# Two transformer layers on one core: output product, offset and pass order at the start of the last feed-forward

## The chip, the cores and the metric

The kernel runs on one core of a Trainium2 chip. The metric is the device time of one execution in microseconds (us), the median of several runs. The profile shows one further execution: TensorE (PE, with its weight loads PEld), VectorE (DVE), ScalarE (ACT), GpSimd (POOL) and the DMA queues, whose issues stand on SP. Times in the profile are counted from the span's start.

## What is computed

Two layers follow one another over x of shape (2, 512, 512), fp32: two independent chunks of 512 rows. Each half-layer adds its result to x and normalises the rows.

```
x = layernorm(x + linear_attention(x))        # elu features against a fixed memory
x = layernorm(x + ternary_ffn(x))             # int8 truncations
x = layernorm(x + softmax_attention(x))       # one head, d = 128, then Wo
x = layernorm(x + ffn(x))                     # inter = silu(x Wg^T) * (x Wu^T); inter Wd^T
```

The change lies where the third line ends and the fourth begins. There, for each chunk b, out = probs V, then x = x + (out Wo) / sums, then the norm over the 512 columns, then products of x with the 1376 rows of Wg and of Wu, and of the result with Wd.

## The kernel before

All of it is unrolled. A chunk b has four tiles t of 128 rows, kept as `xs[b][t]`, 128 x 512. The columns are cut into four blocks k of 128. The 1376 inner columns are eleven weight chunks j, of which the last to be loaded has 96 columns.

**Order.** Each engine runs its own queue in order. The order on GpSimd is that of the program; on the other engines a planner in the compiler lays the instructions out ahead of time, by the program's order and by the times at which it expects each to be ready, and it may move a later instruction into a gap. `tc.issue_after(ins)` ties the instructions of a block behind `ins` on their engine, without a wait of its own. PSUM is one pool of eight banks (`psum`), a bank for each product.

**The end of the softmax attention.** `output(b, t)` is one product of `ots[b]` with `wo1` into a bank (L910; fp32, two instructions). `attended(b, t, p)` adds the bank, scaled by the row sums, to `xs[b][t]` on VectorE (L915). `norm_a1` of chunk 0 takes statistics on VectorE (L155, L157), then `root` makes the reciprocal deviation on GpSimd (L163, L164), then `scalar_norm` makes the offset -mean x rstd in two GpSimd instructions (L904, L905) and applies both on ScalarE (L906). In the program chunk 0's four products and norms come first, then chunk 1's `values`, then chunk 1's four products and additions; chunk 1's statistics come later.

**Splitting the rows.** Full fp32 accuracy is had from products in a reduced format (fp32r): each operand becomes three parts, h (its upper 12 bits, cut by a mask), l (the rest) and d (a cross term). `split_rows(b, room)` does so for x: for each block k it transposes the four tiles into one bank (L942), copies the bank to SBUF on ScalarE (L948; not for block 0 of chunk 0, which is read from the bank), cuts it on VectorE (`cut`, L729), and `row_parts` makes h on ScalarE (L748) and l and d on VectorE (L749, L750). It returns the last instruction as `done`; behind it are tied the statistics of chunk 1's four tiles, and behind these their normalisation on VectorE (L169).

**The products.** `up1(b, j)` makes gate and up for weight chunk j: h and l products gather in a bank `pm`, d products in `pc` (L1007), for each of gate and up. `run` issues them: for j = 0 block by block, since the parts of x come block by block, otherwise first all d, then all h, then all l. `sum_up` evicts on ScalarE (L1017) and VectorE (L1018); a Silu (L1040) and a product (L1042) follow. The steps begin (0,0), (0,1), (0,2), (1,0), (1,1), (1,2); `split_rows(1, ...)` stands behind step (0,1). `down1` (L1082) makes the last product; its norm is `scalar_norm` too, for all tiles but the last.

Of the kernel before, what the change touches and what calls it, by code (L numbers as in the profile page):

```python
# [15 lines left out]
ALU = mybir.AluOpType  # L16
# [3 lines left out]
P = 128  # L20
B, S, HID = 2, 512, 512
NT = S // P
NK = HID // P
# [13 lines left out]
def kernel(  # L37
# [19 lines left out]
    nc = tc.nc  # L57
# [12 lines left out]
    ident = const.tile([P, P], F32, tag="ident", name="ident")  # L70
# [8 lines left out]
    def psum(name):  # L79
        return ps.tile([P, 512], F32, tag="mm", name=name)  # L80


    xs = [[], []]
# [188 lines left out]
    def split(b):  # L272

        hi = xtp.tile([P, NK, S], F32, tag="xt", name=f"xh_{b}").bitcast(F32R)
        los = [pair_tile(f"xl_{b}_{i}").bitcast(F32R) for i in range(2)]
        his = [hi[:, k, :] for k in range(NK)]
        los = [los[k // 2][:, k % 2, :] for k in range(NK)]

        def block(k):
            pt = psum(f"pt_f0{b}_{k}")  # L280
            for t in range(NT):
                nc.tensor.transpose(pt[:, ts(t, P)], xs[b][t][:, ts(k, P)], ident)
            nc.scalar.copy(his[k], pt)
            nc.vector.tensor_sub(los[k], pt, his[k].bitcast(F32))

        return his + los, block
# [12 lines left out]
    with tc.tile_pool(name="a0w", bufs=1) as a0w, tc.tile_pool(name="a0", bufs=2) as a0:  # L299
# [201 lines left out]
        for i, (b, t) in enumerate(order):  # L501
# [10 lines left out]
            if i == 5:  # L512
                parts, block = split(0)
# [21 lines left out]
    with tc.tile_pool(name="f0", bufs=2) as f0:  # L535
# [83 lines left out]
        pds, ys, stats, moved = {}, {}, {}, {}  # L619
# [42 lines left out]
        parts, block = split(1)  # L662
# [62 lines left out]
    def cut(src, w, name):  # L725

        m = cutp.tile([P, 512], F32, tag="cut", name=f"m_{name}")
        p = src.shape[0]
        nc.vector.tensor_single_scalar(  # L729
            m[:p, :w].bitcast(I32), src.bitcast(I32), TOP12, ALU.bitwise_and  # L730
        )
        return m[:p, :w]
# [12 lines left out]
    def row_parts(src, m, parts):  # L745

        h, l, d = parts
        moved = nc.scalar.copy(h, m)  # L748
        nc.vector.tensor_sub(l, src, m)  # L749
        return moved, nc.vector.scalar_tensor_tensor(  # L750
            d, l.bitcast(F32), -BIG, m, ALU.mult, ALU.add
        )


    turn = [6, 7, 8, 9, 10, 0, 1, 2, 3, 4, 5]
# [7 lines left out]
    def take(n):  # L763
        got = free[:n]
        del free[:n]
        return got

    def split_up(j, room):

        c = turn[j]  # L770
        n = CHUNKS[c][1]
        for a in range(2):
            w = gus[c][:, a].rearrange("p k i -> p (k i)")
            up_parts[j, a] = room[3 * a : 3 * a + 3]
            done = weight_parts(w, up_parts[j, a], f"gu{j}_{a}")
        own = wffn.tile([P, 2 * n // P, 512], F32R, tag=f"gu{c}", name=f"ugu_{c}")
        free.extend(units(own))
        return done
# [15 lines left out]
    for b in range(B):  # L794
# [10 lines left out]
        for j in range(2):  # L805
            p = psum(f"pqk_{b}_{j}")
# [6 lines left out]
            moved = nc.scalar.activation(s, p, AF.Identity, bias=bqk[:, j : j + 1])  # L813
# [4 lines left out]
        for t in range(NT):  # L818
            p = psum(f"pv_{b}_{t}")
# [57 lines left out]
    with tc.issue_after(scaled_max.ins):  # L877
        done = split_up(2, room1[6:] + take(4))
# [7 lines left out]
    def values(b, pt, cuts):  # L886

        ot = ot2[:, b, :]
        w = S // cuts
        for i in range(cuts):  # L890
            po = psum(f"pot_{b}_{i}")
            for k in range(NT):
                nc.tensor.matmul(  # L893
                    po[:, :w], qkv[b][2][:, k, :], pt[:, k, ts(i, w)],
                    start=(k == 0), stop=(k == NT - 1),
                )
            (nc.vector.tensor_copy if b else nc.scalar.copy)(ot[:, ts(i, w)], po[:, :w])
        ots.append(ot)

    def scalar_norm(x, stats, name):  # L900

        mv, rstd = stats
        off = small.tile([P, 1], F32, tag="off", name=f"off1_{name}")
        nc.gpsimd.tensor_tensor(off, mv[:, 0:1], rstd, ALU.mult)  # L904
        nc.gpsimd.tensor_scalar(off, off, -1.0, None, ALU.mult)  # L905
        nc.scalar.activation(x, x, AF.Identity, bias=off, scale=rstd)  # L906

    def output(b, t):
        p = psum(f"po1_{b}_{t}")
        nc.tensor.matmul(p, ots[b][:, ts(t, P)], wo1, start=True, stop=True)  # L910
        return p

    def attended(b, t, p):
        x = xs[b][t]
        nc.vector.scalar_tensor_tensor(  # L915
            x, p, probs[b][1][:, t : t + 1], x, ALU.mult, ALU.add
        )
# [6 lines left out]
    def rows_room(b, name):  # L924

        if b == 0:
            tiles = [
                wop.tile([P, 2, 512], F32R, tag="wo", name=f"{name}_{i}") for i in range(6)
            ]
        else:  # L930
            tiles = [
                xtp.tile([P, NK, S], F32R, tag="xt", name=f"{name}_{i}") for i in range(2)
            ] + [wqp.tile([P, 2, 512], F32R, tag="wq", name=f"{name}_{i}") for i in range(2, 4)]
        return [u for t in tiles for u in units(t)]

    def split_rows(b, room):

        parts, moved = [], []
        for k in range(NK):
            pt = psum(f"pt_f1{b}_{k}")  # L940
            for t in range(NT):
                nc.tensor.transpose(pt[:, ts(t, P)], xs[b][t][:, ts(k, P)], ident)  # L942
            if b or k:
                rows = cutp.tile([P, 512], F32, tag="big", name=f"xt_f1{b}_{k}")
                with ExitStack() as tied:
                    if k > 1:
                        tied.enter_context(tc.issue_after(moved[k - 2].ins))
                    nc.scalar.copy(rows, pt)  # L948
                pt = rows
            with ExitStack() as tied:  # L950
                if b == 0 and k == 1:
                    tied.enter_context(tc.issue_after(done.ins))
                m = cut(pt, S, f"x{b}_{k}")
            parts.append(room[3 * k : 3 * k + 3])
            copied, done = row_parts(pt, m, parts[k])
            moved.append(copied)
        return parts, done

    values(0, pt0, 1)
# [2 lines left out]
        attended(0, t, output(0, t))  # L962
        norm_a1(0, t)
    values(1, pt1, 2)
    for t in range(NT):
        attended(1, t, output(1, t))
    rooms = [rows_room(0, "r0"), None]
    x3 = [None, None]
    x3[0], done = split_rows(0, rooms[0])
    stats1 = []  # L970
    for t in range(NT):
        with tc.issue_after(done.ins):
# [10 lines left out]
    def products(b, j, a):  # L983


        n = CHUNKS[turn[j]][1]
        h, l, d = (u[:, : NK * n].rearrange("p (k i) -> p k i", k=NK) for u in up_parts[j, a])
        pc, pm = psum(f"pc_{b}_{j}_{a}"), psum(f"pm_{b}_{j}_{a}")
        passes = [
            [(w[:, k], x3[b][k][i], (pm, pm, pc)[i]) for i, w in enumerate((h, l, d))]  # L990
            for k in range(NK)
        ]
        return pc[:n], pm[:n], passes

    def run(passes, by_block):

        if by_block:
            todo = [p for block in passes for p in block]
        else:
            todo = [block[i] for i in (2, 0, 1) for block in passes]  # L1000
        begun = {}
        for _, _, p in todo:
            begun[id(p)] = begun.get(id(p), 0) + 1
        left = dict(begun)
        for w, x, p in todo:
            n = w.shape[-1]
            nc.tensor.matmul(  # L1007
                p[:n], w, x, start=(left[id(p)] == begun[id(p)]), stop=(left[id(p)] == 1)
            )
            left[id(p)] -= 1  # L1010

    def sum_up(pc, pm):

        n = pc.shape[0]
        ev = evicted.pop(0)
        evicted.append(ev)
        nc.scalar.activation(ev[:n], pc, AF.Copy, scale=CROSS)  # L1017
        nc.vector.scalar_tensor_tensor(ev[:n], pm, MAIN, ev[:n], ALU.mult, ALU.add)  # L1018
        return ev[:n]
# [3 lines left out]
    def up1(b, j):  # L1023

        n = CHUNKS[turn[j]][1]
        g = j // 4
        if (b, g) not in its:
            its[b, g] = fp.tile(
                [P, GROUPS[g], S], F32, tag=f"it{b}{g}", name=f"it_f1{b}{g}", bufs=1
            )  # L1030
            if g == turn.index(last) // 4:
                nc.gpsimd.memset(its[b, g][96:, turn.index(last) % 4, :], 0.0)
        (pc0, pm0, passes0), (pc1, pm1, passes1) = (products(b, j, a) for a in range(2))
        if j == 0:
            run([p + q for p, q in zip(passes0, passes1)], True)
        else:
            run(passes0, False)
            run(passes1, False)
        gate = sum_up(pc0, pm0)
        nc.scalar.activation(gate, gate, AF.Silu)  # L1040
        wide = sum_up(pc1, pm1)
        nc.vector.tensor_mul(its[b, g][:n, j % 4, :], gate, wide)  # L1042
# [156 lines left out]
```

## Time and profile before

| | |
|---|---|
| median of 3 runs | 476.58 us (475.98 to 476.86) |
| the profiled execution | 475.66 us |
| its span, first to last instruction | 473.8 us |
| mean granted TensorE clock | 0.998 |
| TensorE busy, share of the span | 98% |
| start of the first output product of chunk 1 | 278.58 us |
| last row part of chunk 0 (L750) ends | 289.94 us |
| TensorE's second group of transposes starts | 295.79 us |

A line of the timeline has the start, the length, the engine, the line of the program, the operation, what is written and read, and the shapes; in brackets stands how long the engine had been idle and what released it. Several like instructions in a row are one line with a count. A matmul's recorded end lies past the start of the next one, since they are pipelined; the distance of starts is its price.

### The profile page before, as it was taken

The page shows a single profiled execution, that of the slowest core. Times are in us where ns is not written, and L with a number is a line of the kernel's source. Part 1 is how long each engine was busy: PE and PEld are TensorE (multiplying, and loading weights), DVE is VectorE, ACT ScalarE, POOL GpSimd, SP SyncE. Part 2 cuts the span into 40 slices and gives each one's busy share as a digit, 9 for nine tenths or more (in the row PEclk, how much of TensorE's full clock was granted, in tenths as well). Part 3 has the DMA queues.
Part 4 walks back from the last instruction along what each step waited for, and adds up shares of the span by engine and source line. Part 5 has one row for each costly group of instructions (what it writes and reads, how often), then busy time and mean ns, then how long its engine had stood idle before and what let it go on. Part 6 is the DMA issues. An engine that isn't in the chain of part 4 may idle for free.

```text
span 473.8 us, 5817 instructions
## 1 busy us (share of the span) xinstructions
PE 465.8 (98%) x1891; PEld 328.8 (69%) x1891; DVE 349.5 (74%) x688; ACT 272.6 (58%) x513; POOL 115.1 (24%) x147
## 2 busy tenths in 40 slices
PE   9999999999999999999999999999999999999994
PEld 7454444434488788787766567888788888888884
DVE  1355677677766586756989989998875778999852
ACT  3344899556656877546754934786653666334221
POOL 0353102666540293000365032000000000023221
PEclk9999999999999999999999999999999999999999
DMA  8999700000033000231390000000000000001011
GB/s 304 403 347 357 291 1 1 0 0 1 2 121 119 3 1 13 79 91 36 124 381 2 0 1 1 1 1 0 1 0 1 1 1 1 0 24 43 24 46 44
DMA packets 13748, 33.98 MB, mean 72 GB/s; under 512 B 1872, under 2 KB 2768, under 8 KB 13712
## 3 DMA queue, kind: packets, MB, share of 16 engines
q1 hardware_dynamic: 13280, 32.85, 19.1%
q10 hardware_dynamic: 432, 0.66, 0.4%
q8 instruction: 22, 0.36, 0.3%
q14 instruction: 14, 0.11, 0.1%
HBM read 31.40 MB, written 2.10 MB: 71 GB/s over the span
## 4 chain that ended last, share of the span: by engine, by line
PE 71%; ACT 7%; DVE 5%; issue 3%; POOL 1%; POOLq 0%; DVEq 0%; ACTq 0%
PE pm L1007 17%; PE pg_f L550 9%; PE pc L1007 9%; PE pu_f L550 8%; PE pdm L1082 7%; PE pd_f L606 4%; PE pdc L1082 4%; DVE x L412 4%; PE pqk L808 3%; PE po L390 2%; ACT y L403 2%; ACT t L422 2%; PE pv L821 2%; PE po L910 1%; PE pot L893 1%
## 5 line engine op out<-in xcount | busy, mean ns | idle before, releaser
L390 PE MATMUL po<-mw,q 128*128 128x512 f32 x128 | 57.1, 598 | 0.3 <-DVE mv_a L157 0.2
L345 PE MATMUL pq<-xt_a,wq 128*128 128x512 f32 (+1 forms) x136 | 56.4, 568 | 0.0
L163 POOL TENSOR_TENSOR rstd_f<-mv_f,ln_eps 128x1 f32<-128x1 f32 x15 | 4.3, 287 | 183.3 <-DVE mv_f L1093 130.2
L390 PEld LDWEIGHTS po<-mw,q 128*128 128x128 f32 x128 | 23.0, 189 | 32.1 <-issue 18.0
L345 PEld LDWEIGHTS pq<-xt_a,wq 128*128 128x128 f32 x136 | 25.5, 190 | 27.7 <-issue 25.9
L1007 PE MATMUL pm<-r,it_early 128*128 128x512 f32 x144 | 37.4, 390 | 0.4 <-ACT r L748 0.4
L1007 PE MATMUL pm<-r,ugu 128*128 128x512 f32 (+1 forms) x144 | 36.3, 389 | 0.0
L1007 PEld LDWEIGHTS pm<-r,it_early 128*128 128x128 f32 x144 | 27.0, 188 | 6.3 <-ACT r L748 0.7
L412 DVE SCALAR_TENSOR_TENSOR x<-po,den,x 128x511 f32<-128x511 f32 x40 | 29.8, 745 | 1.9
L1007 PEld LDWEIGHTS pm<-r,ugu 128*128 128x128 f32 (+1 forms) x144 | 26.8, 186 | 5.9
L185 ACT ACTIVATE ta_f<-y_f,below_half 128x512 int8<-128x512 f32 (+1 forms) x22 | 15.9, 723 | 23.8 <-DVE y_f L175 23.3
L1018 DVE SCALAR_TENSOR_TENSOR ev_q<-pm,ev_q 128x512 f32<-128x512 f32 (+1 forms) x28 | 19.1, 685 | 13.4 <-PE pm L1007 13.3
L407 POOL TENSOR_TENSOR y<-y,y 128x511 f32<-128x511 f32 x16 | 20.3, 1270 | 31.5 <-ACT y L403 30.7
L576 DVE SCALAR_TENSOR_TENSOR it_f<-tb_f,ta_f 128x512 fp32r<-128x512 int16 (+1 forms) x22 | 15.2, 690 | 16.2 <-ACT tb_f L186 16.2
L351 ACT ACTIVATE e<-pq,bq 128x512 f32<-128x512 f32 x16 | 11.1, 692 | 25.9 <-PE pq L345 25.9
L1007 PE MATMUL pc<-r,ugu 128*128 128x512 f32 (+1 forms) x96 | 25.8, 391 | 0.0
L424 POOL TENSOR_SCALAR td<-wd,inv_down 128x512 fp32r<-128x512 f32 (+1 forms) x11 | 19.5, 1788 | 24.0 <-DVE inv_down L219 23.8
L550 PE MATMUL pg_f<-xh,tu 128*128 128x512 f32 (+1 forms) x88 | 24.8, 402 | 0.0
L550 PE MATMUL pg_f<-xl,tu 128*128 128x512 f32 (+1 forms) x88 | 23.6, 390 | 0.0
L550 PE MATMUL pu_f<-xh,tu 128*128 128x512 f32 (+1 forms) x88 | 23.6, 390 | 0.0
L550 PE MATMUL pu_f<-xl,tu 128*128 128x512 f32 (+1 forms) x88 | 23.6, 389 | 0.0
L1017 ACT ACTIVATE ev_q<-pc 128x512 f32<-128x512 f32 (+1 forms) x28 | 16.4, 590 | 11.5 <-PE pc L1007 11.3
(293 smaller groups left out, 1103.0 us busy)
## 6 DMA issues: line engine op xcount, KB each, us to landing
gu<-in_gu SPq DMA_DIRECT2D x20, 512.0 KB, 8.2
wo<-in_wo SPq DMA_DIRECT2D x16, 512.0 KB, 6.6
wd<-in_wd SPq DMA_DIRECT2D x20, 256.0 KB, 4.6
wq<-in_wq SPq DMA_DIRECT2D x8, 256.0 KB, 4.2
out<-x SPq DMA_DIRECT2D x7, 256.0 KB, 2.0
x<-in_x SPq DMA_DIRECT2D x6, 256.0 KB, 5.3
gu<-in_gu SPq DMA_DIRECT2D x2, 384.0 KB, 6.6
wqkv<-in_wqkv SPq DMA_DIRECT2D x1, 768.0 KB, 10.7
```

The source lines that it names most:

```text
L185: nc.scalar.activation(a[:n], y, AF.Relu, bias=below_half[:n])
L345: nc.tensor.matmul(pq[:, at], wq[h][:, k, :], xt[:, k, at], start=(k == 0), stop=(k == NK - 1),)
L390: nc.tensor.matmul(po, qs[b][h0 + j][:, ts(t, P)], mw[:, h0 + j, :], start=True, stop=True,)
L407: nc.gpsimd.tensor_add(ys[0][:, :LAST], ys[0][:, :LAST], y[:, :LAST])
L412: steps.append(nc.vector.scalar_tensor_tensor(x[:, :LAST], four[j][:, :LAST], d, x[:, :LAST], ALU.mult, ALU.add))
L424: eng.tensor_scalar(out, w, factor, None, ALU.mult)
L550: nc.tensor.matmul(pp[a][:n], t[:, a, i % NK, :n], x2[b][i], start=(i == 0), stop=(i == 2 * NK - 1),)
L606: nc.tensor.matmul(pd, inter[b][c][:n, ts(t, P)], td[c][:n].bitcast(F32R), start=(c == 0), stop=(c == last),)
L1007: nc.tensor.matmul(p[:n], w, x, start=(left[id(p)] == begun[id(p)]), stop=(left[id(p)] == 1))
L1017: nc.scalar.activation(ev[:n], pc, AF.Copy, scale=CROSS)
L1018: nc.vector.scalar_tensor_tensor(ev[:n], pm, MAIN, ev[:n], ALU.mult, ALU.add)
L1082: nc.tensor.matmul(p[:, :w], got[j // 4][1][kind][:n, j % 4], down_parts[j][kind][:, cols], start=(j == 0 and kind == kinds[0]), stop=(j = ...
```

## The change

Three edits.

- `scalar_norm`: the offset is made by one GpSimd `tensor_scalar`, mean times rstd times -1.
- `split_rows` gets an argument `behind`, two functions. With it, all sixteen transposes are issued first, the blocks tied in order; behind the last of them comes the first function, `output(1, 3)`; and behind block 0's last part on VectorE comes the second, `attended(1, 3, p)`. The loop over chunk 1's tiles ends one earlier. Only chunk 0's call passes `behind`; chunk 1's transposes go on as before.
- For j = 0, the gate's and up's passes of a block alternate: h of gate, h of up, l, l, d, d, where they were h, l, d of gate and then h, l, d of up. This holds for both chunks.

```diff
         mv, rstd = stats
         off = small.tile([P, 1], F32, tag="off", name=f"off1_{name}")
-        nc.gpsimd.tensor_tensor(off, mv[:, 0:1], rstd, ALU.mult)
-        nc.gpsimd.tensor_scalar(off, off, -1.0, None, ALU.mult)
+        nc.gpsimd.tensor_scalar(off, mv[:, 0:1], rstd, -1.0, ALU.mult, ALU.mult)
         nc.scalar.activation(x, x, AF.Identity, bias=off, scale=rstd)
...
-    def split_rows(b, room):
-
-        parts, moved = [], []
+    def split_rows(b, room, behind=None):
+
+
+        parts, moved, pts = [], [], []
+
+        def turn(k):
+            pt = psum(f"pt_f1{b}_{k}")
+            with ExitStack() as tied:
+                if behind and k:
+                    tied.enter_context(tc.issue_after(pts[k - 1][1].ins))
+                for t in range(NT):
+                    turned = nc.tensor.transpose(
+                        pt[:, ts(t, P)], xs[b][t][:, ts(k, P)], ident
+                    )
+            pts.append((pt, turned))
+
+        if behind:
+            for k in range(NK):
+                turn(k)
+            with tc.issue_after(pts[-1][1].ins):
+                p = behind[0]()
         for k in range(NK):
-            pt = psum(f"pt_f1{b}_{k}")
-            for t in range(NT):
-                nc.tensor.transpose(pt[:, ts(t, P)], xs[b][t][:, ts(k, P)], ident)
+            if not behind:
+                turn(k)
+            pt = pts[k][0]
             if b or k:
...
             copied, done = row_parts(pt, m, parts[k])
             moved.append(copied)
+            if behind and k == 0:
+                with tc.issue_after(done.ins):
+                    behind[1](p)
         return parts, done
...
-    for t in range(NT):
+    for t in range(NT - 1):
         attended(1, t, output(1, t))
     rooms = [rows_room(0, "r0"), None]
     x3 = [None, None]
-    x3[0], done = split_rows(0, rooms[0])
+    t = NT - 1
+    x3[0], done = split_rows(
+        0, rooms[0], (lambda: output(1, t), lambda p: attended(1, t, p))
+    )
...
         if j == 0:
-            run([p + q for p, q in zip(passes0, passes1)], True)
+            run([[x for y in zip(p, q) for x in y] for p, q in zip(passes0, passes1)], True)
         else:
```

## The prediction

> **What bounds the kernel now.** I read the page's first part, then the chain of work that ended last, then the timeline of each engine around the change.
>
> ```profile
> PE 465.8 (98%) x1891; PEld 328.8 (69%) x1891; DVE 349.5 (74%) x688; ACT 272.6 (58%) x513; POOL 115.1 (24%) x147
> PE 71%; ACT 7%; DVE 5%; issue 3%; POOL 1%; POOLq 0%; DVEq 0%; ACTq 0%
> ```
>
> TensorE is busy for 98% of the span. So only a stretch in which TensorE stands still can be shortened by reordering, and the chain says where it does: cut to the neighbourhood of the change, in order of time, it leaves TensorE once.
>
> ```profile
> 278.74 3.43 PE po L910 x8
> 282.17 0.12 PE pt_f L942
> 282.30 0.73 DVE x L915
> 283.03 0.61 DVE m_x L729
> ...
> 283.66 0.70 DVE r L749
> ...
> 284.39 0.70 DVE r L750
> ...
> 285.13 0.50 PE pc L1007
> ```
>
> The columns are start, length, and who. The fourth output product ends, VectorE adds it to x (L915), and only then does it cut the first transposed block (L729, L749, L750), for which the feed-forward's first products wait. TensorE's own timeline shows what that costs:
>
> ```profile
> 282.01 1.91 PE L942 MATMUL pt_f<-ident,x 128*128 128x128 f32 x16
> 284.33 0.73 PE L1007 MATMUL pm<-r,it_early 128*128 128x512 f32 x2 [0.41 <-ACT r L748]
> 285.13 0.50 PE L1007 MATMUL pc<-r,it_early 128*128 128x512 f32 x1
> 285.47 0.62 PE L1007 MATMUL pm<-r,it_early 128*128 128x512 f32 x2
> 285.94 0.62 PE L1007 MATMUL pc<-r,it_early 128*128 128x512 f32 x2
> 286.40 1.55 PE L1007 MATMUL pm<-r,it_early 128*128 128x512 f32 x6
> ```
>
> The chain also gives the pace of a dense stream: 8 products in 1.81 to 1.82 us, 0.227 each; 16 transposes in 1.75, 0.109 each; 8 halves of an output product in 3.43, 0.429 each. So the transposes are issued by 282.01 + 1.75 = 283.76 and the first product starts 0.57 later; the seven products before 286.40 would need 1.59 and take 2.07, 0.48 lost, mostly before the product that reads L750's result. Together 1.05 us. From 286.40 to the end of the down products I find no other stop above 0.25 us. **1.05 us is the ceiling.** 0.2% of 476.58 is 0.95 us, about what a measurement of this kernel can tell from no change.
>
> Before that, the fourth norm of chunk 0 is made by GpSimd and ScalarE:
>
> ```profile
> 279.79 0.19 POOL L163 TENSOR_TENSOR rstd_a<-mv_a,ln_eps 128x1 f32<-128x1 f32 x1
> 280.06 0.57 POOL L164 TENSOR_TENSOR rstd_a<-rstd_a,minus_half 128x1 f32<-128x1 f32 x1
> 280.71 0.19 POOL L904 TENSOR_TENSOR off_a<-mv_a,rstd_a 128x1 f32<-128x1 f32 x1
> 280.99 0.22 POOL L905 TENSOR_SCALAR off_a<-off_a 128x1 f32<-128x1 f32 x1
> 281.24 0.81 ACT L906 ACTIVATE x<-x,off_a,rstd_a 128x512 f32<-128x512 f32 x1 [0.56 <-POOL off_a L905]
> ```
>
> x is ready at 282.05, and the transposes start at 282.01: close, hidden by the output product. And 13 us later comes a second meeting of the two chunks:
>
> ```profile
> 294.03 0.55 DVE L169 TENSOR_SCALAR x<-x,mv_a,rstd_a 128x512 f32<-128x512 f32 x1 [0.44 <-POOL rstd_a L164]
> 295.02 0.55 DVE L169 TENSOR_SCALAR x<-x,mv_a,rstd_a 128x512 f32<-128x512 f32 x1 [0.44 <-POOL rstd_a L164]
> 295.79 1.91 PE L942 MATMUL pt_f<-ident,x 128*128 128x128 f32 x16
> ```
>
> The last tile of chunk 1 is normalised at 295.57, and its first transpose (the fourth of 16) is due at 295.79 + 3 x 0.109 = 296.12. That is 0.55 of slack, about 0.45 after the weight load ahead of it.
>
> **The Trainium skill.** "TensorE: Matmul & The Clock Gate", section "LDWEIGHTS (loading the stationary operand)", gives columns / 1.2 ns: 107 ns for 128. The trace agrees in an indirect way: after a wait the second product starts 0.335 after the first, 0.108 over the pace, so a stop costs its length and one uncovered load. "GPSIMD Engine Reference", "Key points", says that GpSimd shares SBUF interfaces with VectorE and suffers from VectorE instructions with two SBUF inputs. The trace agrees: L904 takes 0.19 in this stretch but 2.28 at 441.8, beside such instructions. "VectorE: DVE Perf Modes", "The perf-mode tier table", puts a PSUM source in a slower tier for tensor_scalar: the cut L729 takes 0.68 from PSUM, 0.42 from SBUF, so block 0 keeps the dear one.
>
> **The change, part by part.**
>
> 1. Offset in one GpSimd step. L904 and L905 take 0.28 each from start to start. One tensor_scalar with a per-partition factor has no row here; the nearest is L905, 0.22. Bounds: 0.22, or the old pair, 0.53. I take 0.23, so 0.28 less in each norm. Norms 1 to 3 queue behind one another on GpSimd: norm 1 begins at 277.03 (statistics), then 277.03 + 3 x 1.11 gives 280.36 for the last offset, L906 from 280.42 to 281.23, 0.82 earlier. If the step took 0.53, x would stay at 282.05 and the transposes would lose 0.57 against part 2.
>
> 2. Output product (1,3) behind the transposes. TensorE does the same work, in another order: transposes from 282.01 - 0.86 = 281.15; block 0's fourth at 281.48 finds x ready (281.23); all by 282.90; the product by 283.76. No DMA moves, SP's queue is untouched, and GpSimd only has fewer instructions. VectorE: the third L915 ends at 282.17, so the cut starts at 282.08 instead of 282.95 (0.87 earlier); ScalarE's copy is ready at 283.41, L749 at 283.50, L750 at 284.21. TensorE is free at 283.76, later than the first two, so the 0.57 goes. L915 for (1,3) is put behind L750: 284.13 to 284.86. Behind it on VectorE wait the cuts of blocks 1 to 3: the first at 284.78 instead of 285.00. **So of VectorE's 0.87 only 0.22 is left for everything after block 0.**
>
> 3. Passes by kind (h,h,l,l,d,d for gate and up, where it was h,l,d,h,l,d). Four products, 0.91, now lie before the first d: due at 284.67, ready at 284.21. That takes the other 0.48. In chunk 1 the parts were ready anyway (d of block 0 at 301.03, used from 303.5); gate's last product moves back by two, 0.45, ahead of an eviction that nothing is waiting for then. Cost nothing; without that cover, 0.45.
>
> What is late next: TensorE has done block 0's six products at 285.12, and block 1's h comes at 285.00 - 0.22 + 0.42 + 0.65 = 285.85. That is 0.73, three products of the next weight chunk (their parts for block 0 exist; the plan put two such in gaps before, at 286.17 and 289.16). Block 3's h, at 289.15 - 0.22 = 288.93, leaves another 0.3. With none of these gaps filled, the last of chunk 0's 24 products ends where it does now and the gain is nil; with two fillers 0.43; with five the whole 1.05.
>
> Then the second meeting. If TensorE runs 1.05 ahead, the fourth transpose is due at 295.07; the tile is normalised at 295.57 - 0.22 = 295.35, and with the load's 0.1 TensorE can't be further ahead than 0.45 + 0.22 = 0.67. The plan orders by its own times; it left VectorE's two 0.44 holes before L169 unfilled although evictions were ready, so it seems to take these norms as sooner than they are, and will put the transposes there without other products ahead. **I take 0.65 us**: 475.66 - 0.65 = 475.01 for the profiled execution (span 473.8, 1.86 around it). That execution lies 0.92 below the median of the runs, 476.58; on it the same gain gives 475.9.
>
> **Rivals.**
>
> A. Everything is filled, at the second meeting too (the next chunk's cross products need only chunk 0's parts): gain 0.95 to 1.05, 475.6. For it: the plan filled gaps before. Against it: VectorE's holes.
>
> B. The gaps behind block 0 stay open, because L915 took the place of the wait that it left: gain 0 to 0.4, 476.4. For it: VectorE is behind block 0 nearly as late as now. Against it: fillers exist and PSUM banks are free (transposes 0 to 2 are read by 284.8).
>
> C. Slower. VectorE has no idle moment from 295.0 to 323.9. In it chunk 1's parts are cut 2.0 to 2.4 us before their use; with TensorE 0.65 ahead and VectorE 0.22, 1.6 to 2.0 is left. If the plan, seeing chunk 0's results sooner, lets evictions and gate products go ahead of these cuts, each costs 0.6. Up to three are free; six cost 3.6 - 1.8 = 1.8 of stall, less the 0.65: 477.7. It decides from the fifth on (3.0 - 1.8 - 0.65 = 0.55 slower). Against it: the cuts stand earlier in the program than the evictions that would be freed.
>
> **How the numbers follow.** The forecast 0.38, A 0.34, B 0.11, C 0.17. A reaches the bound of 0.95 us only narrowly: three quarters of it count as faster, with a quarter of the forecast, since the median of three runs scatters by about 0.3: 0.255 + 0.095 = 0.35. Slower is C, nearly whole: 0.16. The rest, 0.49, is within 0.2%. The range takes in A, the forecast and B with 0.4 of scatter between runs: 475.1 to 477.0; C lies outside.
>
> **What would show it.** TensorE's first product at 283.8 without a wait named; L915 once between L750 and the second L729; L905 gone, L904 one instruction of 0.2 to 0.25, the fourth L906 at 280.4. If cross products lie between 285.1 and 285.9, part 2 is filled. If the second transposes start near 295.0 with a stop inside the first four, the forecast; with products of the third chunk ahead of them, A. A first product later than 284.0, or L906 after 281.5, makes the prediction wrong; so does any new wait of TensorE on VectorE between 296 and 324.

## The result, and the profile after

| | before | after |
|---|---|---|
| median of 22 runs each | 476.47 us (475.62 to 476.91) | 475.29 us (474.34 to 477.18) |
| ratio, 95% interval | | 0.9978 (0.9971 to 0.9985) |
| profiled execution | 475.66 us | 474.57 us |
| its span | 473.8 us | 472.8 us |
| granted TensorE clock | 0.998 | 0.999 |

By the ratio the kernel became 1.05 us faster (0.71 to 1.38 by its interval); the two medians differ by 1.18. Forecast were 475.9 us and a gain of 0.65. The sign holds, and so does the mechanism in the stretch around the change; the amount was too small by about 0.4. The page's first part and the shares of the chain say hardly more than that TensorE is still the bound (behind POOL there are eleven instructions less, one for each norm made by ScalarE):

```profile
PE 465.6 (98%) x1891; PEld 328.6 (70%) x1891; DVE 349.5 (74%) x688; ACT 272.5 (58%) x513; POOL 112.7 (24%) x136
...
PE 72%; ACT 7%; DVE 5%; issue 3%; POOL 0%; POOLq 0%; DVEq 0%; ACTq 0%
```

The chain of work around the change, in order of time (start, length, who), no longer leaves TensorE. Where VectorE's L915, L729, L749 and L750 stood in it, there are now the fourth output product and the first products:

```profile
281.27 1.75 PE pt_f L946 x16
283.02 0.86 PE po L909 x2
283.88 0.92 PE pm L1030 x4
284.80 0.69 PE pc L1030 x3
285.50 0.23 PE pm L1030
285.72 0.23 PE pc L1030
285.95 1.84 PE pm L1030 x7
```

The timeline of the same stretch gives the steps one by one (its starts lie about 0.16 ahead of the chain's; the lines moved: L906 is now L905, L910 is L909, L915 is L914, L942 is L946, L1007 is L1030, L1018 is L1041, L1082 is L1105):

```profile
280.18 0.26 POOL L904 TENSOR_SCALAR off_a<-mv_a,rstd_a 128x1 f32<-128x1 f32 x1
280.48 0.81 ACT L905 ACTIVATE x<-x,off_a,rstd_a 128x512 f32<-128x512 f32 x1 [0.32 <-POOL off_a L904]
281.11 1.91 PE L946 MATMUL pt_f<-ident,x 128*128 128x128 f32 x16
282.05 0.68 DVE L729 TENSOR_SCALAR m_x<-pt_f 128x512 int32<-128x512 int32 x1
283.49 0.69 DVE L750 SCALAR_TENSOR_TENSOR r<-r,m_x 128x512 fp32r<-128x512 f32 x1
284.10 0.74 DVE L914 SCALAR_TENSOR_TENSOR x<-po,sums,x 128x512 f32<-128x512 f32 x1
284.76 0.75 DVE L729 TENSOR_SCALAR m_x<-xt_f 128x512 int32<-128x512 int32 x2
285.33 0.39 PE L1030 MATMUL pm<-r,it_early 128*128 128x512 f32 x1
285.56 0.39 PE L1030 MATMUL pc<-r,it_early 128*128 128x512 f32 x1
285.88 1.90 PE L1030 MATMUL pm<-r,it_early 128*128 128x512 f32 x7
```

Before, the cuts of block 0 and of the next two blocks were these:

```profile
282.95 0.68 DVE L729 TENSOR_SCALAR m_x<-pt_f 128x512 int32<-128x512 int32 x1
285.00 0.75 DVE L729 TENSOR_SCALAR m_x<-xt_f 128x512 int32<-128x512 int32 x2
```

x is ready at 281.29, before the fourth transpose (281.11 + 3 x 0.109 = 281.44). The cut starts at 282.05, 0.90 earlier than before; the cuts of the other blocks start at 284.76, 0.24 earlier, because L914 lies between. Block 0's six products and one of the next weight chunk run from 283.72 (the start of the output product's second half, 283.29, and its 0.43) to 285.33, then two more of that chunk; the starts 285.33, 285.56, 285.88 are 0.23 and 0.32 apart and the next one 0.34 behind, so the wait for block 1's h costs 0.10 + 0.11 over the pace of 0.227.

Ten microseconds later the second meeting stands in the timeline of GpSimd, VectorE and TensorE:

```profile
292.90 0.85 POOL L164 TENSOR_TENSOR rstd_a<-rstd_a,minus_half 128x1 f32<-128x1 f32 x1
294.78 0.55 DVE L169 TENSOR_SCALAR x<-x,mv_a,rstd_a 128x512 f32<-128x512 f32 x1 [0.44 <-POOL rstd_a L164]
294.91 2.12 PE L946 MATMUL pt_f<-ident,x 128*128 128x128 f32 x16
296.78 1.17 PE L1030 MATMUL pc<-r,ugu 128*128 128x512 f32 x4
```

The last tile is normalised at 295.33, the fourth transpose was due at 294.91 + 0.33 = 295.24. Sixteen transposes take 296.78 - 294.91 = 1.87 where 1.67 lay between the same starts before (295.79 to 297.46): 0.2 is lost. The product behind the transposes before was

```profile
297.46 1.17 PE L1007 MATMUL pc<-r,ugu 128*128 128x512 f32 x4
```

TensorE comes 0.88 ahead of before and leaves 0.68 ahead; 0.04 of both is an earlier start ahead of the change. From there on it stays 0.67 to 0.70 ahead to its last product.

In the executions compared below, chunk 1's first output product starts anywhere between 278.54 and 280.11, so two stretches are used in place of the span: the **distance** from the start of chunk 1's first output product to the start of TensorE's last product, and the **tail** from there to the end of the span. Before: 188.92 and 6.33. After: 188.26 and 6.00. So 0.66 of the gain lies where the prediction looked, and 0.33 at the very end, where it didn't look. Together 0.99 in one execution each, against 1.05 by the runs.

### The profile page after: what moved, and what is told of

Its sections match the earlier page's. It is cut to its first block, busy times and chain, and to the rows that moved or that the text cites. A ratio compares the mean times of both kernels' runs of the same rounds, so it can differ in the third digit from the quotient of the medians.

```text
span 472.8 us, 5810 instructions
## 1 busy us (share of the span) xinstructions
PE 465.6 (98%) x1891; PEld 328.6 (70%) x1891; DVE 349.5 (74%) x688; ACT 272.5 (58%) x513; POOL 112.7 (24%) x136
## 4 chain that ended last, share of the span: by engine, by line
PE 72%; ACT 7%; DVE 5%; issue 3%; POOL 0%; POOLq 0%; DVEq 0%; ACTq 0%
PE pm L1030 17%; PE pg_f L550 9%; PE pc L1030 8%; PE pu_f L550 8%; PE pdm L1105 7%; PE pd_f L606 4%; PE pdc L1105 4%; DVE x L412 4%; PE pqk L808 3%; PE po L390 2%; ACT y L403 2%; ACT t L422 2%; PE pv L821 2%; PE po L909 1%; PE pot L893 1%
## 5 line engine op out<-in xcount | busy, mean ns | idle before, releaser
L1030 PE MATMUL pm<-r,it_early 128*128 128x512 f32 x144 | 36.9, 392 | 0.0
L1030 PE MATMUL pm<-r,ugu 128*128 128x512 f32 (+1 forms) x144 | 36.3, 389 | 0.0
L1030 PEld LDWEIGHTS pm<-r,it_early 128*128 128x128 f32 x144 | 27.0, 188 | 6.4 <-ACT r L748 0.7
L1030 PEld LDWEIGHTS pm<-r,ugu 128*128 128x128 f32 (+1 forms) x144 | 26.8, 186 | 5.9
L1041 DVE SCALAR_TENSOR_TENSOR ev_q<-pm,ev_q 128x512 f32<-128x512 f32 (+1 forms) x28 | 19.1, 684 | 13.3 <-PE pm L1030 13.3
L1030 PE MATMUL pc<-r,ugu 128*128 128x512 f32 (+1 forms) x96 | 25.8, 390 | 0.0
```

Source lines behind the costliest of these rows:

```text
L1030: nc.tensor.matmul(p[:n], w, x, start=(left[id(p)] == begun[id(p)]), stop=(left[id(p)] == 1))
```

## The experiments

Four questions: what each part does alone and in pairs, what sets the cap at the second meeting, whether L914 can be moved out of the way of blocks 1 to 3, and what the 0.33 at the end is. The kernels were timed in three groups, each with its own runs of before (medians 476.48, 476.50, 476.32). In the expectations, theory M is the prediction's account, with the second meeting as the cap, and the other letters are its rivals. In the table "gain" is the shortening of the distance.

| kernel | gain, us | tail, us | ratio (95%) |
|---|---|---|---|
| after | 0.66 | 6.00 | 0.9978 (0.9971 to 0.9985) |
| after, again (b3_after) | 0.91 | 6.00 | 0.9973 (0.9961 to 0.9985) |
| 1 alone (a1_offset) | 0.06 | 6.00 | 0.9992 (0.9984 to 1.0000) |
| 2 alone (a3_move) | 0.07 | 6.32 | 1.0001 (0.9993 to 1.0009) |
| 3 alone (a2_order) | 0.44 | 6.32 | 0.9996 (0.9985 to 1.0006) |
| 2 and 3 (a4_no_offset) | 0.10 | 6.34 | 0.9998 (0.9990 to 1.0007) |
| 1 and 2 (b1_no_order) | 0.63 | 6.01 | 0.9981 (0.9973 to 0.9989) |
| 1 and 3 (b2_no_move) | 0.46 | 6.00 | 0.9986 (0.9975 to 0.9997) |
| after, later meeting (b4_meet) | 0.86 | 6.01 | 0.9976 (0.9969 to 0.9982) |
| after, late addition (c1_late_add) | 0.69 | 6.00 | 0.9981 (0.9972 to 0.9989) |
| after, padded (d1_pad) | 0.64 | 6.31 | 0.9981 (0.9974 to 0.9988) |
| later meeting and addition (e1_meet_add) | 0.75 | 6.00 | 0.9981 (0.9973 to 0.9988) |

The intervals of the ratios are 0.6 to 1.2 us wide, so what tells neighbours apart is the trace, with one execution each.

**The parts alone.** The offset in one step, in the kernel before:

```diff
-        nc.gpsimd.tensor_tensor(off, mv[:, 0:1], rstd, ALU.mult)
-        nc.gpsimd.tensor_scalar(off, off, -1.0, None, ALU.mult)
+        nc.gpsimd.tensor_scalar(off, mv[:, 0:1], rstd, -1.0, ALU.mult, ALU.mult)
```

> The kernel before with the offset in one GpSimd step, nothing else. Measured by the distance from the start of chunk 1's first output product to the start of TensorE's last product: 188.92 us before, 188.26 after, a gain of 0.65. Theory M (the gain of the whole change is set by the second meeting, where chunk 1's last norm lets TensorE run only so far ahead, and each part counts only through what it does to that): TensorE does not wait for chunk 0's norm here, so the fourth L906 moves 0.8 earlier and the distance stays within 0.05; ratio of the times 1.000. Rival N (eleven GpSimd instructions fewer are worth something by themselves, which would explain that the runs differ by 1.05 us while the traces show 0.65 in this stretch): the trace shows nothing, and the ratio is 0.9990 to 0.9993.

The gain on the way is 0.06: x is ready sooner, but the transposes stand behind the output product, as before. The shorter tail is nearly all that it brings: 0.39 in all, a ratio of 0.9992. That is where rival N put the runs; theory M had 1.000.

The pass order, in the kernel before:

```diff
-            run([p + q for p, q in zip(passes0, passes1)], True)
+            run([[x for y in zip(p, q) for x in y] for p, q in zip(passes0, passes1)], True)
```

> The kernel before with the alternating pass order alone. Theory M: the stop before L750's result (0.24 and one uncovered load of 0.11) goes, and VectorE's order stays, so at the second meeting TensorE may be 0.42 ahead at most: gain in the distance 0.35 to 0.42. Rival P (each part removes its own stop, and the parts add up to the whole): 0.48 as in the prediction's third step. Rival Q (the pass order does nothing, since a filler could have gone there): 0.

Gain 0.44, a little more than theory M's 0.35 to 0.42 and less than rival P's 0.48. TensorE's timeline of this kernel:

```profile
285.42 1.21 PE L1007 MATMUL pm<-r,it_early 128*128 128x512 f32 x4 [0.41 <-ACT r L748]
286.47 0.85 PE L1007 MATMUL pc<-r,it_early 128*128 128x512 f32 x3
287.16 1.99 PE L1007 MATMUL pm<-r,it_early 128*128 128x512 f32 x8
```

Fifteen products lie between 285.42 and the two d products at 288.99 with 0.16 over the pace (3.57 for 15 x 0.227 = 3.41), little more than the 0.11 of one weight load after the wait; before it was 0.48 over seven. The wait for h (0.41 of idle time) stays, as it must. M's cap was not reached: at the second meeting the last norm ends at 296.68, 0.12 before the fourth transpose (296.80).

The moved product alone: the change of `split_rows` and its call, with the two-step offset and the old `run` line.

> The kernel before with the fourth output product of chunk 1 behind the transposes, alone: offset in two steps, old pass order. Theory M: the transposes begin at 281.1 but their fourth waits for x until 282.1, 0.6 lost; the first block is cut about 0.4 later than in the changed kernel, and all of VectorE behind it, so chunk 1's last norm comes 0.2 later than before the change and the gain is 0.2 (0 to 0.3). Rival P: 0.57, the whole stop before the first product.

Gain 0.07. ScalarE's, TensorE's and VectorE's lines:

```profile
281.36 0.49 PE L947 MATMUL pt_f<-ident,x 128*128 128x128 f32 x3
281.45 0.81 ACT L906 ACTIVATE x<-x,off_a,rstd_a 128x512 f32<-128x512 f32 x1 [0.56 <-POOL off_a L905]
282.32 1.64 PE L947 MATMUL pt_f<-ident,x 128*128 128x128 f32 x13 [0.47 <-ACT x L906]
282.68 0.69 DVE L729 TENSOR_SCALAR m_x<-pt_f 128x512 int32<-128x512 int32 x1 [0.31 <-PE pt_f L947]
```

Three transposes, then 0.47 of waiting for x: the old stop has moved from behind the transposes into them. The starts are 282.32 - 281.36 = 0.96 apart where 0.33 were due, 0.63 lost. Without the offset edit the moved product brings next to nothing. Of the 0.21 by which TensorE is still ahead at the second group of transposes, the second meeting takes 0.15: the sixteen take 1.82 (295.79 to 297.61) instead of 1.67.

**The pairs.** After with the two-step offset again:

```diff
-        nc.gpsimd.tensor_scalar(off, mv[:, 0:1], rstd, -1.0, ALU.mult, ALU.mult)
+        nc.gpsimd.tensor_tensor(off, mv[:, 0:1], rstd, ALU.mult)
+        nc.gpsimd.tensor_scalar(off, off, -1.0, None, ALU.mult)
```

> The changed kernel with the offset in two steps again. Theory M: the fourth transpose waits for x until about 282.1, block 0 is cut about 0.4 later, and chunk 1's last norm with it: gain over the kernel before 0.1 to 0.3 in the distance, so the offset, worth nothing alone, is worth about 0.45 here. Rival P (parts add up): still 0.65, if the offset alone is worth nothing.

0.10, with the same wait of 0.47 before the fourth transpose. TensorE is 0.30 ahead at the second group of transposes and loses 0.24 there. After with the old `run` line:

```diff
-            run([[x for y in zip(p, q) for x in y] for p, q in zip(passes0, passes1)], True)
+            run([p + q for p, q in zip(passes0, passes1)], True)
```

> The changed kernel with the old pass order. Theory M: L750's result is there at 284.2 when the third product is due, so the old order stops TensorE by no more than 0.1, and the second meeting caps the gain as before: 0.6 to 0.65, the pass order worth nothing beside the moved product. Rival P: 0.65 less 0.48, 0.17.

0.63, as much as with the pass order but for 0.02. TensorE:

```profile
283.77 0.91 PE L1030 MATMUL pm<-r,it_early 128*128 128x512 f32 x2
284.57 0.50 PE L1030 MATMUL pc<-r,it_early 128*128 128x512 f32 x1
284.91 0.63 PE L1030 MATMUL pm<-r,it_early 128*128 128x512 f32 x2
```

The output product (L909) starts at 283.19 and holds TensorE for 0.86, to 284.05; two products more end at 284.50; the d product starts at 284.57, 0.06 late, and the next one 0.34 behind, 0.11 over the pace. So the product in the old order waits 0.06 for L750's result, not 0.48: the moved output product gives VectorE the time that the pass order was to give. What it still loses here, the second meeting returns: its sixteen transposes start at 295.36 and the product behind them at 297.12, 1.76 apart, so the stop there is 0.09 where it was 0.20 in after. Without this stop the two would stand at 0.72 and 0.86 (an estimate: each gain with its stop added), so the pass order would be worth some 0.14 if the meeting did not hide it. The kernel with the moved product undone, that is before with the offset and the pass order:

> The kernel before with the offset in one step and the alternating passes, the fourth product where it was. Theory M: as with the pass order alone, gain 0.40 to 0.46 in the distance, the offset adding nothing to it, and 0.33 in the tail: 0.75 in all, ratio 0.9984. Rival P: 0.48 of distance from the order and more from the offset.

0.46, what the pass order gives alone (0.44), and the shorter tail. Alone and in pairs the gains read 0.06, 0.07, 0.44 and 0.63, 0.46, 0.10: they do not add. The offset and the moved product are worth 0.6 together and 0.07 or less singly; the pass order is worth 0.44 without them and, with the second meeting's stop, 0.02 beside them.

**The change again, and the cap.**

> The changed kernel once more. Theory M: distance 188.26 again to 0.02; the runs' ratio comes out nearer 0.9986, which 0.65 us makes, than 0.9978, the rest being scatter. Rival N: 0.9978 again, with the same 0.65 in the trace.

Unchanged, it gained 0.91 on the way this time, where M and N both had 0.65; the ratio, 0.9973, lies on N's side. The same four lines as above, in this execution:

```profile
293.07 0.55 POOL L164 TENSOR_TENSOR rstd_a<-rstd_a,minus_half 128x1 f32<-128x1 f32 x1
294.64 0.55 DVE L169 TENSOR_SCALAR x<-x,mv_a,rstd_a 128x512 f32<-128x512 f32 x1 [0.44 <-POOL rstd_a L164]
295.03 1.91 PE L946 MATMUL pt_f<-ident,x 128*128 128x128 f32 x16
296.70 1.16 PE L1030 MATMUL pc<-r,ugu 128*128 128x512 f32 x4
```

This execution runs 0.15 later (its first output product starts at 278.69, not 278.54). One GpSimd power took 0.55 where it had taken 0.85, so the last norm ends at 295.19, or 0.3 earlier against the first output product; the sixteen transposes take 1.67, the full pace. The cap is where the prediction put it, and whether it holds hangs on 0.3 us of one GpSimd instruction.

If so, moving the transposes behind products that need chunk 0 alone must take the stop away, whatever the power takes:

```diff
+        elif between:
+            run([[block[2]] for block in passes0], True)
+            between()
+            run([[block[i]] for i in (0, 1) for block in passes0], True)
+            run(passes1, False)
...
+    def second():
+        rooms[1] = rows_room(1, "r1")
+        x3[1], _ = split_rows(1, rooms[1])
+
     for i, (b, j) in enumerate(steps):
-        up1(b, j)
-        if i == 1:
-            rooms[1] = rows_room(1, "r1")
-            x3[1], _ = split_rows(1, rooms[1])
+        up1(b, j, second if i == 2 else None)
```

> The changed kernel with chunk 1's transposes put behind the four cross products of the third weight chunk's gate. Theory M: TensorE has 0.91 us of other work when chunk 1's last norm is late, the stop of 0.21 inside the first four transposes goes, and nothing behind it is late: gain 0.86. Rival D (VectorE, without a break from 295 on, is the next limit: chunk 1's parts come later and TensorE waits for them at 302): 0.65 or less.

Gain 0.86:

```profile
293.22 0.85 POOL L164 TENSOR_TENSOR rstd_a<-rstd_a,minus_half 128x1 f32<-128x1 f32 x1
295.09 0.55 DVE L169 TENSOR_SCALAR x<-x,mv_a,rstd_a 128x512 f32<-128x512 f32 x1 [0.44 <-POOL rstd_a L164]
295.21 1.08 PE L1030 MATMUL pc<-r,ugu 128*128 128x512 f32 x4
296.12 1.91 PE L946 MATMUL pt_f<-ident,x 128*128 128x128 f32 x16
```

The power takes the long 0.85, the norm ends at 295.64, and the transposes, from 296.12, run at the pace. What is left of 1.05, 0.19, is about the 0.21 at block 1's h. By the runs this kernel can't be told from after (0.9976 and 0.9978).

**The addition out of the way.** L914 of tile 3 delays the cuts of blocks 1 to 3 by 0.66. It can stand before the statistics that need it:

```diff
             if behind and k == 0:
-                with tc.issue_after(done.ins):
-                    behind[1](p)
+                late.append(p)
...
         with tc.issue_after(done.ins):
+            if t == NT - 1:
+                attended(1, t, late[0])
             stats1.append(layernorm_stats(xs[1][t], f"a11_{t}"))
```

> The changed kernel with chunk 1's fourth addition (L914) between the third and fourth of chunk 1's statistics on VectorE, not behind block 0's parts. Theory M: blocks 1 to 3 are cut 0.65 earlier, the stops of TensorE at 285.6 go, and chunk 1's norms on GpSimd begin 0.65 earlier and end some 0.4 earlier (the plan puts an eviction between), so the second meeting allows 1.0: gain 0.9 to 1.05. Rival D (VectorE's total work up to the last norm is the limit, and that is unchanged): 0.65.

A miss for theory M: 0.69 instead of 0.9 and more, and near rival D's 0.65. Blocks 1 to 3 do come sooner (the second cut starts 5.56 behind the first output product, 6.22 in after), and there is no stop at the meeting. But TensorE stops behind block 0:

```profile
285.37 0.63 PE L1032 MATMUL pc<-r,it_early 128*128 128x512 f32 x2
285.95 1.65 PE L1032 MATMUL pm<-r,it_early 128*128 128x512 f32 x6
287.44 0.74 PE L1032 MATMUL pc<-r,it_early 128*128 128x512 f32 x2
288.02 0.63 PE L1032 MATMUL pm<-r,it_early 128*128 128x512 f32 x2
```

Two products from 285.37 to 285.95 are 0.58 where 0.45 is the pace; six to 287.44 are 1.49 instead of 1.36; two to 288.02 again 0.58. Together 0.39. In after three products of later weight chunks lie in this stretch; here none does. The likeliest reason is that the planner, with these blocks due sooner by its own times, saw no gap to fill; its times were not looked at, so that is argued. On VectorE the plan also put an eviction (L1043, 292.35 to 293.01) ahead of the fourth statistics, so the last norm ends 16.76 behind the first output product (296.02), no sooner to speak of than in after (16.79). That is D's point, and it is the next limit: the fourth transpose, at 296.13, starts only 0.11 behind that norm. Without the stops behind block 0 the gain would have been some 0.80 at most (an estimate: 0.69 + 0.11). The later meeting, with its edit above, and the addition behind block 1's last part:

```diff
-            if behind and k == 0:
+            if behind and k == 1:
                 with tc.issue_after(done.ins):
                     behind[1](p)
```

> The changed kernel with both repairs: chunk 1's transposes behind the third chunk's four cross products, and the fourth addition on VectorE behind block 1's last part, not block 0's. Theory M: the second meeting no longer stops TensorE; what is left are stops behind block 0 that the plan does not foresee, since it takes out the fillers when it sees the parts coming sooner: gain in the distance 0.7 to 0.95, no better than the 0.86 of the first repair alone. Rival D: 1.05, since block 1's parts come 0.65 earlier and nothing else stops TensorE.

0.75, inside what was expected, and no better than the later meeting alone.

**The tail.** The tail is 6.31 to 6.34 in the five executions with 147 GpSimd instructions and 6.00 to 6.01 in the eight with 136. If the number matters and not what they do, eleven empty ones give it back:

```diff
         nc.gpsimd.tensor_copy(mw[:, :, LAST], z)
+        for _ in range(11):
+            nc.gpsimd.memset(fill[0:1, 0:1], 0.0)
```

> The changed kernel with eleven one-element memsets on GpSimd added early, at a time when GpSimd waits for weights; they do nothing for the result. GpSimd has as many instructions again as before the change. In the ten traces so far the time from TensorE's last product to the end of the span is 6.33 us where the offset is made in two steps and 6.00 where it is made in one, and the longer ones fetch one more 8 KB of instructions after the span. Theory F (the length of GpSimd's program decides whether one more fetch stands in the end of the kernel): tail 6.33 us again, the late fetch is back, the distance stays between 188.0 and 188.3, and the ratio goes up by 0.0007 against the changed kernel. Rival (the tail belongs to the norm's own last instructions): tail 6.00.

6.31 again, with the offset still in one step: in the traces the tail follows the number of GpSimd instructions, not what they do in the norm. Only this one number was tried, so it isn't shown whether each instruction counts or a boundary is crossed. The view of the transfers shows one thing that differs. Before, in the stretch from 470 us (queue, number, MB, share):

```profile
q10 hardware_dynamic: 144, 0.13, 3.9%
q1 hardware_dynamic: 144, 0.13, 3.9%
q14 instruction: 1, 0.01, 0.3%
```

The padded kernel, from 471 us:

```profile
q14 instruction: 1, 0.01, 0.2%
```

After, from 468 us, two lines and no third:

```profile
q10 hardware_dynamic: 144, 0.13, 3.3%
q1 hardware_dynamic: 144, 0.13, 3.3%
```

Such a fetch of 8 KB of instructions, at 474.41 in before and at 475.52 in the padded kernel, is found in all five executions with the longer tail and in none of the other eight. But it begins when the span is over (473.82 and 474.69). What lengthens the tail lies ahead of it: GpSimd's last two semaphore steps start 0.39 apart in before, 0.38 in the padded kernel and 0.08 in after. The fetch on record comes too late to be what GpSimd waits for there. What does take these 0.3 us stays open.

The runs bear out the shorter tail where the offset is made in one step: in these eight cases the gain by the runs is 0.15 to 0.39 larger than in the distance, and in the three with the offset in two steps 0 to 0.25 smaller. They do not show that padding brings the tail back: the padded kernel gained 0.91 by the runs, 0.27 more than in the distance, like the short ones. Its interval, 0.57 to 1.24, also takes in the 0.66 that its trace gives. So the padded kernel's longer tail is shown by one trace, and the runs neither confirm nor exclude it.

## Why the prediction was right in kind, and short by 0.4 us

- **The ceiling, 1.05 us of stops**, holds for the stretch: no execution gained more than 0.91 in it.
- **Step 1, the offset.** Taken at 0.23, it took 0.27; norms follow at 1.14 instead of 1.11. x was ready 0.06 later than worked out (281.29 for 281.23), which the 0.15 before the fourth transpose hides. That the old pair would cost the moved product 0.57 is what a3_move and a4_no_offset show, with 0.63 lost.
- **Step 2, the moved product.** Transposes at 281.11 (281.15 forecast), cut at 282.05 (282.08), L914 at 284.10 (284.13), next cut at 284.76 (284.78). Right, the 0.22 left to later blocks as well.
- **Step 3 failed.** "That takes the other 0.48" is true of the kernel before (0.44 alone), not behind step 2: there the d product of the old order would be late by 0.06 and one load (b1_no_order). By the prediction's own times the old order's first d was due two products after 283.76, at 284.21, just when its part was ready. The two steps were each priced against the kernel before, and then added. It did no harm to the sum, since the cap came after it.
- **The fillers** came as forecast, in the stretch between 285.1 and 285.8. That they would leave 0.21 at block 1's h was not in the sum.
- **The second meeting.** The cap of 0.67 is right in mechanism (norm at 295.33, forecast 295.35; the transposes with nothing ahead of them), and 0.65 measured 0.66 in the profiled execution. But it was taken as one number from one execution. It moves by 0.3 with GpSimd's power, and the repeat gained 0.91.
- **The term that the sum had not: the tail, 0.33.** "GpSimd only has fewer instructions" was costed at nothing. It is the larger part of the error; why it arises stays open. 0.66 + 0.33 = 0.99 for one execution of the changed kernel, 0.91 + 0.33 = 1.24 for the other; the runs' 1.05 lies between.
- **Rivals.** A named the right amount, 0.95 to 1.05, for a reason that the profiled execution contradicts: the second meeting does have its stop. B, open gaps behind block 0, falls with the fillers. C, slower, falls too: from 296.8 to the end of the span's products no new wait appears, and TensorE keeps its lead to within 0.03.
- **Range and chances.** The median, 475.29, lies 0.2 inside the range, which was wide enough because it took in rival A, not because of a term for the tail; that part was luck. The likeliest outcome by the stated chances was a change within 0.2% (0.49, against 0.35 for faster). The runs show 0.22%, with an interval from 0.15% to 0.29%, so they don't tell on which side of that line the change lies.

## What to carry over

When several parts of a change bear on one stop, price them in the order in which they act, each against the kernel that the earlier ones leave: here two parts were worth 0.07 or less singly and 0.63 together, and a third fell from 0.44 to 0.02. Follow a gain to the next place where the freed engine meets another stream, and ask how much the durations that set that meeting vary; one execution doesn't say. And count instructions even on an engine with nothing critical to do, since in these traces their number shows at the end of the program.

## What the runs showed of the hardware

- In the traces the end of the program is 0.3 us longer with 147 GpSimd instructions than with 136 (tails of 6.31 to 6.34 and of 6.00 to 6.01), whether the eleven belong to the offsets or are memsets. The Trainium skill, "Runtime: NRT & Kernel Launch", section "Instruction fetch mechanics", says that a sequencer fetches its instructions by a DMA queue of its own, in blocks of 16 KiB. The trace has two queues for instructions alone, without their engines' names: fetches of 16 KB on q8 (22 fetches, 0.36 MB), as the page says, but of 8 KB on q14 (14 fetches, 0.11 MB). No run shows that a fetch makes the tail longer.
- GpSimd's power on 128 x 1 takes 0.55 to 0.85 us in chunk 1's four norms. The Trainium skill, "GPSIMD Engine Reference", section "Key points", has GpSimd share its SBUF interfaces with VectorE. In most executions the long ones lie beside VectorE's L169, and 0.55 is seen beside the statistics (c1_late_add, 292.98). But in b3_after and in e1_meet_add the third power ran beside L169, started 0.10 after it as in after, and took 0.55. What decides is open.
- A stop of TensorE costs its length and 0.11 for the next product, which the prediction reads as one weight load that nothing covers: at block 1's h (0.10 + 0.11) and in b1_no_order (0.06 + 0.11). No run takes the two apart.
